# Attention on one core: later split subtractions on GpSimd, the transfers around the reciprocals issued a step later, the bias products ahead of the first projections

## The chip, the core and the metric

The kernel runs on one core of a Trainium2 chip. A core has TensorE (PE in the profile, matmul), VectorE (DVE), ScalarE (ACT), GpSimd (POOL) and SyncE (SP), which here only starts transfers. Each engine works through its own instructions in order and waits on semaphores for the others. Transfers are started from an engine's queue and carried out by 16 DMA engines. The metric is device time in microseconds of one execution.

## The reference, cut to what matters

Four layers follow each other on an input of 8 images, 256 channels, 32 x 32 pixels. The change lies in the first one, an attention block with an MLP:

```python
y = _bn(xf, g1, b1)                       # batch norm over images and pixels
q = einsum('bcn,oc->bon', y, wq) + bq     # 16 heads, 16 channels each
k = einsum('bcn,oc->bon', y, wk) + bk
v = einsum('bcn,oc->bon', y, wv) + bv     # 16 heads, 64 channels each
attn = softmax(einsum('bhnk,bhkm->bhnm', q, k) / KD ** (-0.5))
o = einsum('bhnm,bhmd->bhnd', attn, v)
o = einsum('bdn,od->bon', o, wp) + bp
xf = xf + o
# then a batch norm, an MLP with relu6 and a residual
```

There are 1024 pixels, so each head of each image has a 1024 x 1024 matrix of scores. The other layers (a deformable convolution, a binary convolution, another deformable convolution) are computed after it by code that the change does not touch.

## The kernel before, in words

**Groups, blocks and steps.** Heads are taken four at a time: a *group* is an image b and a quarter g of the heads, 32 groups in all. A group's queries are halved; a *block* is (b, g, half), 64 in all. A block runs over eight *steps*, one per tile of 128 keys. `step(t)` issues for every t: the scores of the next step and their exponentials (`exps`, L451 and L452), the products of the current step's exponentials with v (`attend`, L463), the running sum of the exponentials on GpSimd (L471 and L473, two instructions of 128 x 1024 a step; none at a block's first key tile), and the search for the largest score of a block 11 steps ahead (`score_max`, L406 products and L410 maxima).

**What else falls into a step.** `plan(step, place, f, ...)` puts a piece of other work into a step at place 0, 1 or 2, and within a place in the order of the calls. The manual schedule holds PE, ACT, DVE and POOL to the written order. SP is not among these engines; its transfers stand in an order that the framework chooses, and the trace shows some of them ahead of ones written earlier.

**Split levels.** The largest score is found from products in bf16. So q and k are each split into three bf16 levels whose sum is the f32 value. `project_qk` (L333 to L349) projects one half of q or k for two groups, copies the result to u (ACT, L346), sends it to DRAM as u_d (L347) and rounds it to level 0 (ACT, L348). `split` then makes, at stage 0, the rest (DVE, L357), at stage 1 level 1 (ACT, L362), and at stage 2 level 2 (DVE, L364); each level goes to DRAM as lev_d (L349, L365). There are four such projections per pair of groups, at steps 8, 10, 12 and 14 of the even group; their stage 2 stands at steps 11, 14, 16 and 18, place 0. The tile u has two buffers and `lev` four. `stack` (L372) gathers levels back from lev_d into sq and sk, 32 transfers per group, half of them for a first pair of heads ("pair 0"); `spread` (L378) brings u_d into q and k.

**Row sums and reciprocals.** When a block has ended (t1_ is its first step after), the sums over keys are made by a product with ones: `total` at t1_ + 3 (L484, copied by ACT at L491). It also starts four transfers that lay the four rows of 512 out as 128 x 16 (L494). `invert` at t1_ + 6 takes the reciprocal (DVE, L497) and sends it to DRAM as inv_d (L499). `lay` at t1_ + 8 reads it back, broadcast over partitions (L506), and `scale` at t1_ + 10 multiplies the block's output on GpSimd (L511). `add_projected` (L541 to L549) projects it and adds it to x. Block 62 has smaller offsets. The last block is done by `total_last` and `scale_last`, with no transfers.

**The largest score.** `enter_max` (L424 to L439) turns a block's maxima into a row of the queries, 11 steps before the block ends, by DVE and four transfers.

**The head.** After the input has landed and its batch norm statistics are made, four normalisations (L315) on DVE, four projections and four v projections are issued, then the splits and stacks of the first group; its two halves of u and its transfers to q and k alternate between SP and POOL. Steps -11 to -4 hold the search for the first block's maxima, which uses f32 products (`score_max_first`, L419, with maxima at L422). `bias(t)` adds the projection of bv to bp: eight products of one column (L305) and an add (L306), for t = 0 and 1. They are planned at steps -6 and -4:

```python
for t in range(2):
    plan(2 * t - 6, 1, bias, t)
```

Of the kernel before, what the change touches and what calls it, by code (L numbers as in the profile page):

```python
# [8 lines left out]
F32 = mybir.dt.float32  # L9
# [9 lines left out]
P = 128  # L19
# [3 lines left out]
HALF = N // 2  # L23
# [135 lines left out]
def conv_seq_kernel(ctx: ExitStack, tc: tile.TileContext, d: dict, out: bass.AP):  # L159
    nc = tc.nc  # L160
# [19 lines left out]
    def col(name, i=0, n=1, p=P):  # L180
        o = COL[name] + i
        return vec[:p, o : o + n]
# [53 lines left out]
    with ExitStack() as s0:  # L236
# [30 lines left out]
        sp = s0.enter_context(tc.tile_pool(name="a_s", bufs=2))  # L267
# [13 lines left out]
        for dst, name, scale in ((bq4, "bq", 4.0), (bk, "bk", 1.0)):  # L281
            ps = ps_p.tile([P, 512], F32, name="pb")
# [12 lines left out]
        def bank():  # L295
            return ps_p.tile([P, 512], F32, name="pb")
# [5 lines left out]
        def bias(t):  # L302
            ps = bank()
            for i in range(8):
                nc.tensor.matmul(ps[:, 0:1], wp[:, i, t * P : (t + 1) * P], bv[:, i : i + 1], start=i == 0, stop=i == 7)  # L305
            nc.vector.tensor_add(bpv[:, t : t + 1], ps[:, 0:1], col("bp", t))  # L306
# [3 lines left out]
        def normed(b, t, h):  # L310
            if t == h == 0:
                ys[b] = yp.tile([P, 2, N], F32, name="y")
            cols = slice(h * HALF, (h + 1) * HALF)
            if b == 0:
                nc.vector.tensor_scalar(ys[b][:, t, cols], x[:, t, b, cols], s1[:, t : t + 1], t1[:, t : t + 1], ALU.mult, ALU.add)  # L315
            else:
                nc.scalar.activation(ys[b][:, t, cols], x[:, t, b, cols], AF.Identity, bias=t1[:, t : t + 1], scale=s1[:, t : t + 1])
# [4 lines left out]
        def project_qk(b, g2, i):  # L322

            if i == 0:
                u_d[b, g2] = ld.tile([2, P, N], F32, name="u_d")
                lev_d[b, g2] = ld.tile([2, 3, P, N], BF16, name="lev_d")
            which, h = QK[i]
            wt, scale, bias = ((wq, 4.0, bq4), (wk, 1.0, bk))[which]
            cols = slice(h * HALF, (h + 1) * HALF)
            ps = bank()  # L330
            for t in range(2):
                for c in range(2):
                    nc.tensor.matmul(  # L333
                        ps[c * 64 : (c + 1) * 64, :], wt[:, t, g2 * P + c * 64 : g2 * P + (c + 1) * 64], ys[b][:, t, cols],
                        start=t == 0, stop=t == 1,
                    )
            if (b, g2) == (0, 0):

                both = ep.tile([P, 2, HALF], F32, name="e")
                u, rest = both[:, 0, :], both[:, 1, :]  # L340
                lev = ap.tile([P, 2, HALF], F32, name="esum").rearrange("p a c -> p (a c)").bitcast(BF16)
                lev = [lev[:, k * HALF : (k + 1) * HALF] for k in range(3)]
            else:
                u = rest = qp.tile([P, HALF], F32, name="u")
                lev = [lp.tile([P, HALF], BF16, name="lev"), None, None]
            nc.scalar.activation(u, ps, AF.Identity, bias=bias[:, g2 : g2 + 1], scale=scale)  # L346
            nc.sync.dma_start(u_d[b, g2][which, :, cols], u)  # L347
            nc.scalar.copy(lev[0], u)  # L348
            nc.sync.dma_start(lev_d[b, g2][which, 0, :, cols], lev[0])  # L349
            parts[i] = u, rest, lev  # L350

        def split(b, g2, i, stage):

            which, h = QK[i]
            u, rest, lev = parts[i]
            if stage == 0:
                nc.vector.tensor_sub(rest, u, lev[0])  # L357
                return
            if lev[stage] is None:
                lev[stage] = lp.tile([P, HALF], BF16, name="lev")  # L360
            if stage == 1:
                nc.scalar.copy(lev[1], rest)  # L362
            else:
                nc.vector.tensor_sub(lev[2], rest, lev[1])  # L364
            nc.sync.dma_start(lev_d[b, g2][which, stage, :, h * HALF : (h + 1) * HALF], lev[stage])  # L365

        def stack(b, g, pair, i, engines=(nc.sync, nc.sync)):
# [110 lines left out]
        rows, inv_d = {}, {}  # L478

        def totals(m):  # L480

            ps = bank()
            for j in range(4):
                nc.tensor.matmul(ps[32 * j : 32 * j + 32, :], ones[:, 0:32], sums[m, j // 2][:, j % 2, :], start=True, stop=True)  # L484
            return ps

        def total(m):

            ps = totals(m)
            row = sp.tile([P, HALF], F32, name="r", bufs=1)  # L490
            nc.scalar.copy(row, ps)  # L491
            rows[m] = sp.tile([P, 16], F32, name="r16")
            for j in range(4):
                nc.sync.dma_start(rows[m][32 * j : 32 * j + 32, :], row[32 * j : 32 * j + 1, :].rearrange("o (p c) -> o p c", c=16))  # L494

        def invert(m):
            nc.vector.reciprocal(rows[m], rows[m])  # L497
            inv_d[m] = ld.tile([4, HALF], F32, name="inv_d")
            nc.sync.dma_start(inv_d[m].rearrange("j (p c) -> (j p) c", c=16), rows[m])  # L499

# [61 lines left out]
        def plan(step, place, f, *args):  # L562
            work.setdefault((step, place), []).append(lambda: f(*args))

        for n, (b, g) in enumerate(groups):
# [14 lines left out]
            if n % 2 == 0 and n + 2 < len(groups):  # L580
                b_, g2 = groups[n + 2][0], groups[n + 2][1] // 2
                for i in range(4):
                    plan(t0 + 8 + 2 * i, 1, project_qk, b_, g2, i)
                    at = t0 + (10, 12, 15, 17)[i]
# [3 lines left out]
        for n, m in enumerate(blocks):  # L588
            b, g, h = m
            t1_ = (n + 1) * NT  # L590
            if m == blocks[-1]:
                plan(t1_, 0, total_last, m)
                plan(t1_ - 4, 0, make_pick)
                for pair in range(2):
                    plan(t1_ + 5 + pair, 0, scale_last, m, pair)
            else:
                plan(t1_ + 3, 1, total, m)
                at = 6 if n + 2 == nblk else 8
                plan(t1_ + (5 if at == 6 else 6), 0, invert, m)
                plan(t1_ + at, 2, lay, m)  # L600
                for pair in range(2):
                    plan(t1_ + at + 2, pair, scale, m, pair)
            for t in range(2):
                at = (7, 10) if m == blocks[-1] else (9, 10) if m == blocks[-2] else (13, 15)
                plan(t1_ + at[t], 1, add_projected, b, g, t, h)
            if m == blocks[-1]:
                plan(t1_ + 1, 0, nc.scalar.activation, w.tile([P, 1], F32, name="root"), eps, AF.Sqrt)
            plan(t1_ - AHEAD, 0, enter_max, m)
        for t in range(2):
            plan(2 * t - 6, 1, bias, t)  # L610

        def step(t):
            ne, nm = divmod(t + 1, NT), divmod(t + AHEAD, NT)
# [18 lines left out]
        with tc.manual_schedule(engines={mybir.EngineType.PE, mybir.EngineType.Activation, mybir.EngineType.DVE, mybir.EngineType.Pool}):  # L632
            for t in range(2):
                for h in range(2):
                    normed(0, t, h)

            nc.scalar.dma_start(wv, d["wvT"].rearrange("(t p) o -> p t o", p=P))
            nc.gpsimd.dma_start(wp, d["wpT"].rearrange("(t p) o -> p t o", p=P))
            nc.gpsimd.dma_start(bv, d["bv"].rearrange("(t p) -> p t", p=P))
            for i in range(4):  # L640
                project_qk(0, 0, i)
                which, h = QK[i]
                for j in range(4):
                    dst = (qs, ks)[which][0][32 * j : 32 * j + KD, h * HALF : (h + 1) * HALF]
                    (nc.gpsimd if j % 2 else nc.sync).dma_start(dst, parts[i][0][j * KD : (j + 1) * KD, :])
                split(0, 0, i, 0)
            for i in range(4):
                project_v(0, 0, i)
                split(0, 0, i, 1)
                split(0, 0, i, 2)  # L650
            for pair in range(2):
                for i in range(8):
                    stack(0, 0, pair, i, (nc.sync, nc.gpsimd))
            for t in range(-AHEAD, steps + 2 * NT):
                step(t)
            assert not work
# [6 lines left out]
    with ExitStack() as s1_:  # L663
# [334 lines left out]
        for b in range(B):  # L998
            r = 100 * b
# [18 lines left out]
            r = 100 * b - 50  # L1018
# [12 lines left out]
            for t in range(NT):  # L1031
# [8 lines left out]
                if t % 2:  # L1040
                    u = t // 2
# [31 lines left out]
    with ExitStack() as s3_:  # L1073
# [55 lines left out]
        def bank3():  # L1129
            return pp.tile([P, 512], F32, name="ps")  # L1130
# [17 lines left out]
            ps=2, pc=1, pd=1, pw=3, pa=1,  # L1148
# [264 lines left out]
        for b in range(B):  # L1413

            r = 100 * b
# [64 lines left out]
            r = 100 * b + 150  # L1480
# [35 lines left out]
        ps = bank3()  # L1516
# [8 lines left out]
    with tc.If(nc.values_load(flag[0:1, 0:1]) > 0):  # L1525
        with ExitStack() as s3_:
# [17 lines left out]
            first = w.tile([P, GK], F32, name="first")  # L1544
# [220 lines left out]
```

## Time and profile before

| what | value |
|---|---|
| median of three runs | 4542.85 us (4538.98 to 4544.85) |
| the profiled execution's own time | 4529.35 us |
| its span, first to last instruction | 4527.5 us |
| PE busy | 4008.4 us, 89% of the span |
| GpSimd busy | 3301.9 us, 73% |
| VectorE busy | 2863.6 us, 63% |
| ScalarE busy | 1874.9 us, 41% |
| L364, third level, on VectorE | 60 in the loop, 1593 ns mean |
| L357, rest, on VectorE | 60 in the loop, 1137 ns mean |
| L511, scaling, on GpSimd | 126, 1335 ns mean |
| L473, running sum, on GpSimd | 762, 2405 ns mean |

The span includes everything from the first instruction to the last. Attention takes from about 37 us to about 2685 us of it. Shares of busy time are averages over stages with different limits. A wait is listed as "engine, what waited, its line, <- who released it, what, its line", with the total time, the number of waits and the longest. An instruction that waits for several semaphores is put down to the last that came. In lists in order of time the first two columns are start and duration; neighbours of one kind are merged ("x10"), and square brackets hold the idle time of the engine before the instruction and what ended it. "SPq" and "POOLq" are the engines' queues, where transfers are issued; the time shown there is that of the issue, not of the transfer.

### The profile page before, as it was taken

What the parts mean: (1) busy time and instruction counts of PE and PEld (TensorE: products, weight loads), DVE (VectorE), ACT (ScalarE), POOL (GpSimd) and SP (SyncE); (2) the same over time, 40 slices, a digit from 0 to 9 for tenths busy, and PEclk for the clock granted to TensorE, in tenths of its full rate; (3) what the DMA queues carried; (4) which work ended last, traced back from release to release, by engine and by line L of the source; (5) the groups of instructions that cost most, each with busy time, mean ns of one, the idle gap of its engine ahead of it and who ended that gap; (6) DMA issues with size and microseconds to landing.
All of it is one profiled execution on the core that took longest, in us unless ns stands there. A gap on an engine that the chain in (4) does not pass through costs nothing.

```text
span 4527.5 us, 59803 instructions
## 1 busy us (share of the span) xinstructions
PE 4008.4 (89%) x20879; PEld 1528.1 (34%) x20879; DVE 2863.6 (63%) x4984; ACT 1874.9 (41%) x3360; POOL 3301.9 (73%) x2011
## 2 busy tenths in 40 slices
PE   6999999999999999999999997767767757899976
PEld 2333333333333333333333333323223222344332
DVE  5666666666666666666666663455455444688885
ACT  2554555555555555555555541122212211534331
POOL 2889888888889888888888863455555453078787
PEclk8999999999999999999999998788888778999978
DMA  5222221121221222122122112222223222100000
GB/s 163 66 60 54 68 71 54 59 76 55 66 67 54 61 71 65 53 63 75 53 64 68 54 50 63 73 84 79 81 85 93 81 86 69 47 10 15 14 15 24
DMA packets 224358, 284.11 MB, mean 63 GB/s; under 512 B 104352, under 2 KB 134576, under 8 KB 223792
## 3 DMA queue, kind: packets, MB, share of 16 engines
q1 hardware_dynamic: 193488, 196.49, 15.0%
q0 software_dynamic: 28720, 77.90, 5.8%
q10 hardware_dynamic: 1840, 5.81, 0.3%
q8 instruction: 168, 2.75, 0.3%
q14 instruction: 142, 1.16, 0.1%
HBM read 214.10 MB, written 64.34 MB: 62 GB/s over the span
## 4 chain that ended last, share of the span: by engine, by line
PE 73%; DVE 6%; another core or an unknown queue 6%; POOL 5%; issue 5%; DMA 2%; ACT 2%; SPq 1%; DVEq 0%; POOLq 0%; ACTq 0%
PE av L463 18%; PE sc L451 11%; PE pb L406 11%; PE pb L389 5%; PE pb L541 5%; PE pm L758 4%; PE po L771 3%; PE pc L1188 3%; PE pb L333 2%; POOL part L1387 2%; PE pc L978 2%; PE pb L484 1%; POOL ws L1331 1%; PE pa L1379 1%
## 5 line engine op out<-in xcount | busy, mean ns | idle before, releaser
L410 DVE TENSOR_REDUCE pm<-pb 128x1 f32<-128x512 f32 x2016 | 1375.7, 688 | 799.2 <-PE pb L406 796.2
L473 POOL TENSOR_TENSOR esum<-esum,e 128x1024 f32<-128x1024 f32 x762 | 1808.7, 2405 | 58.7 <-ACT e L452 57.5
L452 ACT ACTIVATE e<-sc 128x512 f32<-128x512 f32 x2048 | 1056.9, 602 | 653.2 <-PE sc L451 647.4
L463 PE MATMUL av<-e,v 128*64 128x512 f32 x4096 | 1051.1, 593 | 0.0
L891 POOL DMA_INDIRECT g<-table,idx x576 | 550.0, 955 | 551.2 <-DVE near_p L913 253.9
L406 PE MATMUL pb<-sk,sq 128*64 128x512 bf16 x4032 | 769.0, 387 | 42.8 <-ACT u L346 19.8
L451 PE MATMUL sc<-q,k 32*128 32x512 f32 x4096 | 591.4, 641 | 0.0
L406 PEld LDWEIGHTS <-sq 128*64 128x64 bf16 x4032 | 247.6, 109 | 877.6 <-issue 844.6
L471 POOL TENSOR_TENSOR esum<-e 128x1024 f32<-128x1024 f32 x127 | 303.1, 2406 | 277.7 <-ACT e L452 277.7
L758 PE MATMUL pm<-y,wide 128*128 128x512 f32 x512 | 262.3, 657 | 141.3 <-ACT hid L763 112.4
L463 PEld LDWEIGHTS av<-e,v 128*64 128x64 f32 x4096 | 289.9, 137 | 239.9 <-issue 146.9
L1387 POOL TENSOR_TENSOR part<-part,pr 128x512 f32<-128x512 f32 x212 | 276.0, 1302 | 55.0 <-DVE pr L1370 43.9
L1370 DVE TENSOR_TENSOR pr<-pw,v 128x512 f32<-128x512 f32 x394 | 253.8, 682 | 61.7 <-POOL part L1387 31.8
L1188 PE MATMUL pc<-xpad,wc 128*128 128x512 f32 x576 | 276.4, 605 | 5.3 <-ACT h L1193 5.3
L771 PE MATMUL po<-hid,w 128*128 128x512 f32 x512 | 241.9, 618 | 5.1 <-issue 4.0
L541 PE MATMUL pb<-o,wp 128*64 128x512 f32 x1024 | 244.7, 597 | 0.5 <-DVE r L519 0.3
L451 PEld LDWEIGHTS sc<-q,k 32*128 32x128 f32 x4096 | 164.4, 183 | 231.1 <-issue 187.3
L389 PE MATMUL pb<-wide,y 128*64 128x256 f32 x2048 | 241.8, 379 | 0.0
L763 ACT ACTIVATE hid<-pm,vec 128x512 f32<-128x512 f32 x128 | 87.1, 686 | 311.8 <-PE pm L758 140.8
L765 DVE TENSOR_SCALAR hid<-hid 128x512 f32<-128x512 f32 x128 | 53.1, 432 | 253.1 <-ACT hid L763 222.3
L758 PEld LDWEIGHTS pm<-y,wide 128*128 128x128 f32 x512 | 104.0, 210 | 279.7 <-issue 153.1
L913 DVE TENSOR_TENSOR near_p<-g,near_p 128x320 f32<-128x320 f32 (+1 forms) x384 | 177.4, 462 | 13.2
(259 smaller groups left out, 3981.7 us busy)
## 6 DMA issues: line engine op xcount, KB each, us to landing
sq<-lev_d SPq DMA_DIRECT2D x512, 64.0 KB
r<-inv_d SPq DMA_DIRECT2D x252, 128.0 KB
sk<-lev_d SPq DMA_DIRECT2D x496, 64.0 KB
lev_d<-lev SPq DMA_DIRECT2D x180, 128.0 KB
u_d<-u SPq DMA_DIRECT2D x60, 256.0 KB
g<-table,idx POOLq DMA_INDIRECT x576
table<-v SPq DMA_DIRECT2D x32, 256.0 KB
out<-res SPq DMA_DIRECT2D x32, 256.0 KB
```

The costliest lines, as they stand in the source:

```text
L389: nc.tensor.matmul(ps[c * 64 : (c + 1) * 64, (mt % 2) * 256 : (mt % 2 + 1) * 256], ys[b][:, t, k0 : k0 + 64], wv[:, t, g * 256 : (g + 1) * ...
L406: nc.tensor.matmul(ps[c * 64 : (c + 1) * 64, :], sq[pair][:, c, q0 : q0 + 64], sk[pair][:, c, kh * HALF : (kh + 1) * HALF], start=True, st ...
L410: nc.vector.tensor_reduce(maxima[m][:, pair, qt, kh : kh + 1], ps, AX.X, ALU.max)
L451: nc.tensor.matmul(ps, k[r, kt * P : (kt + 1) * P], q[r, h * HALF : (h + 1) * HALF], start=True, stop=True)
L452: nc.scalar.activation(es[m, kt, j // 2][:, j % 2, :], ps, AF.Exp)
L463: nc.tensor.matmul(av[i * HD : (i + 1) * HD, :], vss[b, g][:, kt, j * HD : (j + 1) * HD], e[:, i, :], start=kt == 0, stop=kt == NT - 1,)
L473: eng.tensor_add(sums[m, pair], sums[m, pair], es.pop((m, kt, pair)))
L541: nc.tensor.matmul(ps[c * 64 : (c + 1) * 64, :], wp[:, 2 * g + i, o0 : o0 + 64], outs[(b, g, h), i], start=i == 0, stop=i == 1,)
L758: nc.tensor.matmul(ps, w1[:, t, i * P : (i + 1) * P], ys[b, h][:, t, :], start=t == 0, stop=t == 1)
L771: nc.tensor.matmul(pss["o", b, h, t], w2[:, j, t * P : (t + 1) * P], hids[b, h, j], start=j == 0, stop=j == 7)
L891: nc.gpsimd.indirect_dma_start(out=g[:, k, :], out_offset=None, in_=tables[b][:TR, :], in_offset=bass.IndirectOffsetOnAxis(ap=idxs[b][:, t ...
L1188: nc.tensor.matmul(S["c", b, h], wc[:, t, k, :], tap(xpads[t], k, H // 2, h * H // 2), start=t == k == 0, stop=t == 1 and k == 8,)
```

## The change

Stage 2 of every split (the subtraction that makes level 2) runs on GpSimd. For the first pair of groups alone, stage 0 does too. `total` now ends with ACT's copy; the four row transfers are in a new function, `narrow`, planned a step later, at t1_ + 4, place 2. `invert` ends with the reciprocal; its transfer to DRAM is in a new function, `put`, planned a step before `lay`, at t1_ + 7, place 2 (t1_ + 5 for block 62). `invert` and `lay` keep their steps. The two calls of `bias` are made in the head, after the transfers of the weights are issued and ahead of the first projection.

```diff
@@ split
+            first = (b, g2) == (0, 0)
             if stage == 0:
-                nc.vector.tensor_sub(rest, u, lev[0])
+                (nc.gpsimd if first else nc.vector).tensor_sub(rest, u, lev[0])
                 return
...
             else:
-                nc.vector.tensor_sub(lev[2], rest, lev[1])
+                nc.gpsimd.tensor_sub(lev[2], rest, lev[1])
@@ total, invert
         def total(m):
             ps = totals(m)
-            row = sp.tile([P, HALF], F32, name="r", bufs=1)
-            nc.scalar.copy(row, ps)
+            rows[m] = sp.tile([P, HALF], F32, name="r", bufs=1)
+            nc.scalar.copy(rows[m], ps)
+
+        def narrow(m):
+            row = rows[m]
             rows[m] = sp.tile([P, 16], F32, name="r16")
             for j in range(4):
                 nc.sync.dma_start(rows[m][32 * j : 32 * j + 32, :], row[32 * j : 32 * j + 1, :].rearrange("o (p c) -> o p c", c=16))
 
         def invert(m):
             nc.vector.reciprocal(rows[m], rows[m])
+
+        def put(m):
             inv_d[m] = ld.tile([4, HALF], F32, name="inv_d")
             nc.sync.dma_start(inv_d[m].rearrange("j (p c) -> (j p) c", c=16), rows[m])
@@ the plan of a block
                 plan(t1_ + 3, 1, total, m)
                 at = 6 if n + 2 == nblk else 8
+                plan(t1_ + 4, 2, narrow, m)
                 plan(t1_ + (5 if at == 6 else 6), 0, invert, m)
+                plan(t1_ + at - 1, 2, put, m)
                 plan(t1_ + at, 2, lay, m)
@@ after the blocks
-        for t in range(2):
-            plan(2 * t - 6, 1, bias, t)
@@ the head
             nc.gpsimd.dma_start(bv, d["bv"].rearrange("(t p) -> p t", p=P))
+            for t in range(2):
+                bias(t)
             for i in range(4):
                 project_qk(0, 0, i)
```

## The prediction

> **What bounds the kernel now.** I read the windows of the span first, then who waited for whom on TensorE (PE), then the instructions in order of time around each kind of wait, and last the head. In the windows (microseconds; busy time and instruction count of PE, its weight loads, VectorE, ScalarE, GpSimd; granted clock; DMA share; GB/s) two stretches of the attention stage stand for all of it:
>
> ```profile
> 400.00:800.00 400.00, 394.59 (x2530) 141.69 (x2528) 262.99 (x430) 211.12 (x398) 351.76 (x159) 1.00 0.22 63
> 800.00:1600.00 800.00, 786.01 (x5032) 282.26 (x5030) 530.38 (x857) 423.07 (x797) 700.63 (x314) 1.00 0.22 62
> ```
>
> PE is busy 98.3% of the 800 us at full clock, so nothing but PE's own gaps can be won there: 14 us in 800. GpSimd is next, 88%, and the change gives it more. PE's waits between 90 and 2560 us (total, times, longest):
>
> ```profile
> PE pb L406 <- ACT u L346: 19.8, 15, 1.4
> PE pb L406 <- DMA sk<-lev_d: 10.2, 7, 1.8
> PE pb L406 <- DMA sq<-lev_d: 9.7, 7, 1.5
> PE pb L406 <- DMA q<-u_d: 1.3, 1, 1.3
> ```
>
> That is one wait of each of two kinds in each of the 15 pairs of head groups (163 us a pair): A, a score product waits for the copy of a projection (19.8 us in all), and B, it waits for stacked levels to land (21.2 us). How A comes about, in the pair that starts near 297 us (start, duration, what, and in brackets the idle time before it and its releaser):
>
> ```profile
> 310.39 24.53 POOL L473 TENSOR_TENSOR esum<-esum,e 128x1024 f32<-128x1024 f32 x10
> ...
> 329.83 2.88 DVE L364 TENSOR_TENSOR lev<-u,lev 128x512 bf16<-128x512 f32 x1
> 332.80 0.69 ACT L346 ACTIVATE u<-pb,bq 128x512 f32<-128x512 f32 x1 [3.97 <-DVE lev L364]
> 333.54 0.41 PE L406 MATMUL pb<-sk,sq 128*64 128x512 bf16 x2 [1.36 <-ACT u L346]
> ```
>
> The fourth projection's u takes the buffer (two of them) that the second split still reads at L364, and L364 takes 2.88 us. It is not the work that takes so long:
>
> ```profile
> L364 DVE TENSOR_TENSOR lev<-u,lev x60: 800/1526/2898, 155.5 to 2470.5; 128x512 bf16<-128x512 f32 x60
> L364 DVE TENSOR_TENSOR esum<-e,esum x4: 692/693/694, 49.2 to 54.4; 128x512 bf16<-128x512 f32 x4
> ```
>
> (min/median/max ns.) The four of the head, where GpSimd adds nothing, take 0.69 us; those beside its adds up to 2.9. B, in the same pair:
>
> ```profile
> 359.75 2.46 SPq L494 DMA_DIRECT2D r<-r  x4
> 362.26 0.58 SPq L372 DMA_DIRECT2D sq<-lev_d  x1
> 362.89 0.42 SPq L372 DMA_DIRECT2D sk<-lev_d  x1
> ...
> 365.65 0.41 PE L406 MATMUL pb<-sk,sq 128*64 128x512 bf16 x2 [1.40 <-DMA sq<-lev_d]
> ```
>
> SyncE's queue (SPq) stood from 356.6 to 359.75 for the totals (row of L491), issued their four transfers, and only then the last two of the 16 stacks of pair 0, which PE needs at 364.25. In the head, VectorE's maxima of the first block:
>
> ```profile
> 70.02 0.68 DVE L422 TENSOR_REDUCE pm<-sc 128x1 f32<-128x512 f32 x1
> 72.92 0.16 DVE L306 TENSOR_TENSOR bpv<-pb,vec 128x1 f32<-128x1 f32 x1 [2.22 <-PE pb L305]
> 74.92 0.69 DVE L422 TENSOR_REDUCE pm<-pb 128x1 f32<-128x512 f32 x1 [1.84 <-PE sc L419]
> ```
>
> Maxima otherwise follow each other at 0.60 us within a step and 1.05 between steps. Each of the two bias products, 3.5 us of PE, opens a gap of 4.90.
>
> **The skill beside it.** The page "SBUF — State Buffer", section "Who interferes with whom", says that a VectorE instruction with two SBUF inputs shares a read port with a GpSimd instruction that reads SBUF, and that the later one waits for the whole of the earlier. The rows of L364 agree: 2.88 is 0.69 plus most of one 2.32 us add, and the ten adds took 24.53 where ten clean ones take 23.2. The forecast goes by the rows. The rule says the move to GpSimd takes L364 out of that contest, while the other subtraction, L357, stays in it. For the price of a subtraction on GpSimd, "GPSIMD Engine Reference", section 3.1, gives about 2.6 cycles an element, 1.1 us for 512 at 1.2 GHz (an estimate from that page) without dispatch; the trace has a nearer row, below, which I use.
>
> **Third-level subtractions on GpSimd (60 in the loop).** No GpSimd instruction with a bf16 operand and two inputs is in the trace. The nearest is the scaling L511: 128x512, two f32 inputs, min 1.254, median 1.270 us. I take 1.25. From below 1.1 (the page); from above 2.4, the price of a 128x1024 add, if mixed types halve the rate (a bf16 memset of 2304 elements takes 2.02 us and an f32 one of 1152 takes 1.06, so memset shows no such penalty). Walk GpSimd's queue in the pair above, with clean adds of 2.32: the adds of key tile 3 run 310.39 to 315.03; subtraction 0 to 316.28; tile 4 to 320.92, plus 0.45 for L357 (the 1.35 us excess of ten adds over three such VectorE instructions) is 321.37; tile 5 to 326.01; tile 6 to 330.65; subtraction 1 to 331.90. So u starts at 331.9 rather than 332.80. PE was ready at 332.18 and u takes 0.69 with 0.05 to be seen, so 331.44 would be early enough: 0.48 of the 1.36 us stays and 0.88 goes. Fourteen pairs give 12.3 and the first, whose wait was 0.78 and whose GpSimd queue has no scaling in it, all 0.78: **13 us of A's 19.8**. Each 0.1 us on the subtraction costs 0.2 us a pair, as two stand ahead of u. Subtraction 2 falls into the 5.42 us in which GpSimd waits for the next block's exponentials, free. Subtraction 3 stands behind the adds of tile 2, near 352.2 where L364 ended near 354.0; the scalings behind it move by 1.25 and the block's last add by the same, into 4.5 us of idle before the next block. The exponentials' buffers (six tiles, three steps) come free 5 us or more before they are wanted. The 120 us of added queue is thus hidden but for the 0.48.
>
> **Row transfers and reciprocals.** SP is not held to the written order; the trace shows it ordered by readiness, with written order as the tie-break (stacks written after the totals stand before them). With the four row transfers written after step 3's stacks, the last two stacks go out at about 356.6, right behind the four before them, and land some 2 us after their issue, 4 us or more before PE wants them: **B goes, 21 us**. The rows then go out at 359.75 or a microsecond later, land by 363, and the reciprocal comes near 374.4: 11 us of cover. The output of the reciprocals (L499) stood in front of ten stacks of pair 1 and held the queue for it; a step later it stands behind them. The broadcast reads (L506) must wait for it to land, about 2 us. In the first block of a pair they went at 302.11, behind the next projection's u_d, and 302.11 + 2.67 + 2 is 306.8 against the scaling at 307.47: cover 0.7 us, the thinnest in the change. The write of the reciprocals now follows the stacks at about 295.2 and lands by 297.5, still before 301, so I price it at nothing. No instruction on VectorE moves: the reciprocal keeps its place, only its transfer is later.
>
> **Head.** Taking the bias products out closes 4.90 - 0.60 = 4.30 and 4.90 - 1.05 = 3.85: 8.15 us. Put ahead of the projections, their weights have landed (GpSimd's queue q0 moved its last bytes by 20 us); the two PSUM banks come free at 31.3 (L288), so two times 3.5 us of PE lie between 31.3 and 38.3, where PE waited until 37.01 for VectorE. Their adds (L306) come behind the four normalisations that end at 38.23, so the first projection starts near 38.4, 1.4 us later. It ran at half pace at first (eight products 3.7 us, later eight 1.9): if the bias products already wake the clock the delay comes back, if not it stays. I take half: **7.4 us** net. The first-level subtractions of the head and its GpSimd transfers now share one queue (four of 1.25, four pairs of transfers of 1.0), ending about 1 us later than before; the stacks then land near 74, wanted near 77. DVE, freed of both, starts its maxima no later than before.
>
> **Sum.** 13 + 21 + 7.4 = 41 us. The profiled execution took 4529.35 us (span 4527.5); it would take 4488. It lies 13.5 below the median of the runs, 4542.85; 41 off that median gives **4502**.
>
> **Rivals.** 1, the tie stays: the totals remain ahead of the last stacks because in the chosen order subtraction 3 on GpSimd counts as late. For it: the third level of q does hang on that subtraction. Against it: it is done 2 us earlier. B stays, 41 - 21 = 20: 4522. 2, the subtraction costs 1.6 to 2.4 us. A's wait is then 1.2 to 2.8 us a pair: gain 41 - 2 x 15 x (0.35 to 1.15) = 30 to 6, so 4512 to 4536. 3, slower: the broadcast reads slip behind the second projection's u_d (310.28) since they now hang on a later write. They would go at 311, 9 us later, land at 315.6, and GpSimd, in order, stands at the scaling for 8 us with all of the block's adds and two subtractions behind it; u and PE follow by as much. 15 x 8 - 41: +79, 4622. It decides from a slip of 0.7 + 41/15 = 3.4 us on. Against it: a whole projection stands between, and before the change the reads never slipped that far. 4, the gains are eaten by new small waits: 4543.
>
> **Chances.** Forecast 0.60 (its own range 4490 to 4513, from 1.1 to 1.5 us a subtraction and 6.5 to 9 in the head); rival 1 0.13; rival 2 0.10; rival 4 0.05; rival 3 0.12. The measurement tells 0.2% (9 us) from no change. Faster 0.83, same 0.05, slower 0.12. The range, 4488 to 4530, takes in rival 1 and most of 2.
>
> **What would show it.** Right: PE's waits on u fall to some 7 us, those on sq and sk to near nothing; a GpSimd group of 64 subtractions at 1.25 us; L422's maxima without the two gaps. Wrong: GpSimd idle in front of its scalings for DMA; subtractions over 1.6 us; row transfers still in front of the last two stacks.

## The result and the profile after

The changed kernel is slower: 4603.25 us median of 4 runs (4597.26 to 4606.04) against 4542.62 for the kernel before on the same chip (4 runs, 4538.98 to 4544.85). The ratio is 1.0132, with an interval of 1.0115 to 1.0150. The forecast was 4502.

The loss arises in attention. The first product of the MLP (L758 before, L768 after) starts at 2690.9 us before and at 2750.8 after, 59.9 later; the medians differ by 60.6. (The two profiled spans, 4527.5 and 4595.5 us, differ by 68.0; the other 8 us lie in the layers behind attention.) Line numbers move with the edit: L365 becomes L367 (a level's transfer to DRAM), L364 becomes L366 (its subtraction), L439 becomes L441 (the row of maxima into q, "q<-line"), L451 becomes L453 (score products of `exps`), L494 becomes L499 (row transfers).

PE's waits of after between 90 and 2560 us (total, times, longest):

```profile
PE sc L453 <- DMA q<-line: 42.6, 15, 3.1
```

That is the whole list. Waits A and B, the two kinds that the prediction was about, are gone entirely. One new kind is there, again once in each of the 15 pairs: the score products of a new block wait for the row of maxima that `enter_max` puts into q. In the window of after from 800 to 1600 us, beside the one shown of before, PE is as busy as it was (785.51 of 800 us), yet does fewer products (4890 for 5032) at a mean granted clock of 0.98 for 1.00:

```profile
800.00:1600.00 800.00, 785.51 (x4890) 281.19 (x4888) 491.38 (x813) 413.97 (x775) 697.55 (x327) 0.98 0.21 62
```

The reason stands in SP's queue. First the kernel before, in order of time, in the pair that starts near 297 us:

```profile
324.54 0.86 DVE L432 STREAM_TRANSPOSE line<-nm 32x32 f32<-32x32 f32 x4
324.98 2.82 SPq L439 DMA_DIRECT2D q<-line  x4
...
331.04 1.14 PE L451 MATMUL sc<-q,k 32*128 32x512 f32 x8
...
332.73 0.34 SPq L365 DMA_DIRECT2D lev_d<-lev  x1
```

The row goes out as soon as VectorE has made it, and the second projection's level 2 goes out 8 us later, when its subtraction is done. Now the same place in the kernel after:

```profile
320.79 9.93 SPq L367 DMA_DIRECT2D lev_d<-lev  x2
...
323.28 0.86 DVE L434 STREAM_TRANSPOSE line<-nm 32x32 f32<-32x32 f32 x4
...
329.23 1.15 POOL L366 TENSOR_TENSOR lev<-u,lev 128x512 bf16<-128x512 f32 x1
329.47 0.38 PE L408 MATMUL pb<-sk,sq 128*64 128x512 bf16 x2
...
330.81 2.82 SPq L441 DMA_DIRECT2D q<-line  x4
...
332.70 4.15 PE L453 MATMUL sc<-q,k 32*128 32x512 f32 x8 [2.85 <-DMA q<-line]
...
336.79 0.64 PE L408 MATMUL pb<-sk,sq 128*64 128x512 bf16 x2
...
337.21 1.92 PE L465 MATMUL av<-e,v 128*64 128x512 f32 x4
```

The two transfers of L367 now stand ahead of the four of L441 in SP's order. The second of them carries the level that GpSimd makes, behind its running sums, at 329.23 to 330.38. So the row, complete at 324.14, leaves from 330.81 on. PE's next products in order after 329.85 are the score products. It waits 2.85 us for the first transfer to land, then starts them two by two as the four transfers arrive, and each runs at half pace (1.05 to 1.19 us instead of 0.59 to 0.69). By both the eight take 4.15 us, where they take 1.14 together otherwise. The products behind them are slow too (0.64 for two that usually take 0.41, 1.92 for four that usually take 1.02). The granted clock shows why: it is 0.50 from the end of the wait to about 339.1, so 6.8 us of each pair's 167 run at half pace, which is the drop of the mean to 0.98. Windows of after, columns as above:

```profile
325.00:329.85 4.85, 4.85 (x30) 1.48 (x24) 2.71 (x5) 2.06 (x4) 4.85 (x3) 1.00 0.00 0
332.70:339.00 6.30, 6.29 (x16) 2.69 (x18) 0.69 (x1) 2.39 (x4) 2.27 (x1) 0.50 0.37 111
```

SP's own waits show the held transfer without a timeline. Of before:

```profile
SPq L365 <- DVE lev L364: 105.2, 44, 3.8
SPq L365 <- DVE r L497: 57.6, 15, 4.1
```

The second row is, by the times of the pair near 297 us, projection 1's level: the reciprocal that VectorE makes just behind its subtraction came last by the profile. The two together are 162.8 us in 59 waits. Of after:

```profile
SPq L367 <- POOL lev L366: 237.5, 60, 9.2
```

### The profile page after: what moved, and what is told of

It is laid out like the page before. It is cut to its first block, busy times and chain, and to the rows that moved or that the text cites. A ratio compares the mean times of both kernels' runs of the same rounds, so it can differ in the third digit from the quotient of the medians.

```text
span 4595.5 us, 59727 instructions
## 1 busy us (share of the span) xinstructions
PE 4066.4 (88%) x20879; PEld 1547.1 (34%) x20879; DVE 2780.2 (60%) x4916; ACT 1881.0 (41%) x3360; POOL 3348.0 (73%) x2079
## 4 chain that ended last, share of the span: by engine, by line
PE 73%; another core or an unknown queue 7%; POOL 6%; DVE 5%; issue 5%; ACT 2%; DMA 1%; SPq 0%; DVEq 0%; POOLq 0%; ACTq 0%
PE av L465 19%; PE sc L453 13%; PE pb L408 11%; PE pb L391 5%; PE pb L548 5%; PE pm L768 3%; PE pc L1198 3%; PE po L781 3%; POOL part L1397 2%; PE pb L333 2%; PE pc L988 1%; PE pb L486 1%; DVE near_p L923 1%; POOL ws L1341 1%
## 5 line engine op out<-in xcount | busy, mean ns | idle before, releaser
L475 POOL TENSOR_TENSOR esum<-esum,e 128x1024 f32<-128x1024 f32 x762 | 1788.8, 2380 | 62.9 <-ACT e L454 62.4
L465 PE MATMUL av<-e,v 128*64 128x512 f32 x4096 | 1066.6, 602 | 0.0
L453 PE MATMUL sc<-q,k 32*128 32x512 f32 x4096 | 636.4, 653 | 42.6 <-DMA q<-line 42.6
L768 PE MATMUL pm<-y,wide 128*128 128x512 f32 x512 | 260.1, 652 | 145.8 <-ACT hid L773 121.0
L453 PEld LDWEIGHTS sc<-q,k 32*128 32x128 f32 x4096 | 186.6, 186 | 286.5 <-issue 197.8
L768 PEld LDWEIGHTS pm<-y,wide 128*128 128x128 f32 x512 | 102.6, 208 | 283.2 <-issue 146.1
L988 PE MATMUL pc<-xb,ws 128*128 128x512 bf16 x504 | 132.0, 421 | 71.0 <-ACT ac L999 36.2
```

What stands on the lines that cost most here:

```text
L453: nc.tensor.matmul(ps, k[r, kt * P : (kt + 1) * P], q[r, h * HALF : (h + 1) * HALF], start=True, stop=True)
L465: nc.tensor.matmul(av[i * HD : (i + 1) * HD, :], vss[b, g][:, kt, j * HD : (j + 1) * HD], e[:, i, :], start=kt == 0, stop=kt == NT - 1,)
L475: eng.tensor_add(sums[m, pair], sums[m, pair], es.pop((m, kt, pair)))
L768: nc.tensor.matmul(ps, w1[:, t, i * P : (i + 1) * P], ys[b, h][:, t, :], start=t == 0, stop=t == 1)
```

## The experiments

The theory (T) after reading the traces: the loss is the place of one transfer in SP's queue. Projection 1's level 2 waits for GpSimd, and the row of maxima waits behind it. Rivals: the row transfers that now go out later push something else back (X); or GpSimd's added work itself holds up the rest, whatever SP's order (G).

The runs come from several chips, on which the layers after attention run at different granted clocks (0.85 in `before` and 0.94 in `bias`, from 2800 to 4150 us); the kernel before takes 4543, 4211 or 4528 us. The expectations of `bias`, `xfer`, `split` and `poolq` give whole times, to be read as differences from 4543. Each time below is a difference from the kernel before on the same chip, and beside it stands the start of the MLP's first product in that run's trace, which marks the end of attention (2690.9 before, 2750.8 and 2755.4 in two profiles of after).

| kernel | us against before | ratio and interval | end of attention |
|---|---|---|---|
| `bias`: bias products alone | -5.4 | 0.9988 (0.9981 to 0.9995) | 2684.5 |
| `xfer`: row transfers alone | -23.7 | 0.9946 (0.9929 to 0.9962) | 2666.8 |
| `split`: subtractions alone | +84.6 | 1.0202 (1.0185 to 1.0219) | 2777.6 |
| `again`: the change once more | +59.8 | 1.0122 (1.0092 to 1.0153) | 2755.4 |
| `nosplit`: the change without the subtractions | -29.0 | 0.9931 (0.9914 to 0.9947) | 2661.1 |
| `only_i1`: before, one subtraction of four moved | +68.1 | 1.0163 (1.0146 to 1.0180) | 2757.8 |
| `poolq`: the change, one transfer in GpSimd's queue | -37.9 | 0.9911 (0.9895 to 0.9928) | 2652.5 |
| `actq`: the change, that transfer in ScalarE's queue | -48.6 | 0.9882 (0.9866 to 0.9899) | 2641.8 |
| `i1_dve`: the change, one subtraction back on VectorE | -48.0 | 0.9890 (0.9874 to 0.9907) | 2641.1 |
| `dose`: the change, that one subtraction done twice | +98.1 | 1.0186 (1.0144 to 1.0228) | 2777.9 |

### The three parts alone

`bias` is the kernel before with this edit:

```diff
-        for t in range(2):
-            plan(2 * t - 6, 1, bias, t)
...
+            for t in range(2):
+                bias(t)
             for i in range(4):
                 project_qk(0, 0, i)
```

> The kernel before with one edit of the change: the bias products ahead of the first projections. Nothing in the loop over pairs differs, the transfer to q<-line stands in SP's queue as before. Every theory expects the same here, 4535 us (4533 to 4538): the first score product of exps came 7.7 us earlier in the changed kernel (83.06 against 90.78 us), and that carries to the end. If it shows 4540 or more, the head's gain does not reach the end, and the loss in the loop is smaller than reckoned.

Measured: -5.4 us, at the edge of what was expected. The first score product of `exps` starts at 85.5 us, not at 82.99 as in the changed kernel: alone, the edit wins 5.3 us there. The expectation had set down to it all that the changed kernel gains there, 7.8 us (its 83.06 is the time at which a list of the chain of work has that step; the product itself starts at 82.99).

`xfer` is the kernel before with `narrow` and `put`:

```diff
-            row = sp.tile([P, HALF], F32, name="r", bufs=1)
-            nc.scalar.copy(row, ps)
+            rows[m] = sp.tile([P, HALF], F32, name="r", bufs=1)
+            nc.scalar.copy(rows[m], ps)
+
+        def narrow(m):
+            row = rows[m]
...
+        def put(m):
...
+                plan(t1_ + 4, 2, narrow, m)
...
+                plan(t1_ + at - 1, 2, put, m)
```

> The kernel before with one edit of the change: narrow and put, the transfers around the reciprocals, issued a step later. Theory T (the loss is the level transfer of projection 1, which now waits for GpSimd ahead of the q<-line transfer in SP's queue): the subtractions are still on VectorE, so nothing is lost, and wait B (21.2 us in the kernel before) goes: 4521 us (4515 to 4530). Rival X (the later transfers push the loads of the next pair back): 4600 us or more, with the wait of the score product on q<-line in this trace too. Rival G (GpSimd's added load) expects the same as T here.

Measured: -23.7 us. PE's waits on sq and sk are gone, A is there as before (19.8 us in 15 waits), q<-line does not show. X is out.

`split` is the kernel before with the subtractions moved:

```diff
-                nc.vector.tensor_sub(rest, u, lev[0])
+                (nc.gpsimd if first else nc.vector).tensor_sub(rest, u, lev[0])
...
-                nc.vector.tensor_sub(lev[2], rest, lev[1])
+                nc.gpsimd.tensor_sub(lev[2], rest, lev[1])
```

> The kernel before with one edit of the change: the split's late subtractions on GpSimd. Theory T: all of the loss is here. 15 pairs lose about 7.2 us each at the score product that waits for q<-line (108 us) and win wait A (13 to 20 us): 4543 + 108 - 17 = 4634 us, 4620 to 4640; with B still there one of the two waits may shorten the other, which is why the low end is 4620. Rival X: 4525 us, as forecast for the subtractions alone. Rival G (POOL busier, whatever the order of SP's queue): 4620 to 4640 as T; the next kernel parts these two.

Measured: +84.6 us, inside the expected +77 to +97; the loss is in this part. PE's largest wait between 80 and 2720 us:

```profile
PE sc L452 <- DMA q<-line: 44.3, 16, 3.3
```

A is gone here, and half of B as well (10.9 us of 19.9 are left in its waits on sq and sk); PE comes later to it.

> The changed kernel itself, beside which the next one is read. The parts measured alone were -5.4 us (bias products), -23.7 (row transfers) and +84.6 (subtractions); if they add up, 55.5 us above the kernel before, 50 to 62.

Measured: +59.8 us, where the three parts add up to 55.5, inside the interval of 42 to 69 us. The parts are not quite independent: `split` and `xfer` both shorten B.

> The changed kernel with all subtractions back on VectorE: bias products and row transfers as changed. If the parts add up: the 5.4 us of the bias products alone and the 23.7 us of the row transfers alone, 29 us below the kernel before (24 to 33).

`nosplit` has the edits of `bias` and `xfer` together. Measured: -29.0 us, as expected, with A still there (19.7 us).

### Order of the queue, or load of GpSimd

`only_i1` moves a quarter of the work, in the kernel before:

```diff
-                nc.vector.tensor_sub(lev[2], rest, lev[1])
+                (nc.gpsimd if i == 1 and (b, g2) != (0, 0) else nc.vector).tensor_sub(lev[2], rest, lev[1])
```

> The kernel before with one subtraction of the four on GpSimd: projection 1's level 2. The head and the row transfers are as before. SP's order of issue flips as in the changed kernel: projection 1's level-2 transfer ahead of q<-line. Theory T: nearly the whole loss of the split with a quarter of its work on GpSimd: 70 to 105 us above the kernel before. Rival G: a quarter of the split's +85, about +20.

Measured: +68.1 us (61 to 76 from the interval), at the low end of what T expects (just under its 70) and over three times what G does. SP's queue of this kernel (the list ends at 340 us, with three of the row's four transfers):

```profile
328.59 9.50 SPq L365 DMA_DIRECT2D lev_d<-lev  x2
...
336.58 1.16 POOL L364 TENSOR_TENSOR lev<-u,lev 128x512 bf16<-128x512 f32 x1
...
338.18 2.13 SPq L439 DMA_DIRECT2D q<-line  x3
```

It is the pattern of after with one GpSimd subtraction a pair. PE's wait on q<-line is 33.0 us in all (2.2 a pair), 11 less than in `split`, where more subtractions stand in GpSimd's queue; that is 11 of the 16.5 us between the two kernels.

`i1_dve` is the complement: in the changed kernel the same one goes back, the other three stay on GpSimd.

```diff
-                nc.gpsimd.tensor_sub(lev[2], rest, lev[1])
+                (nc.vector if i == 1 and not first else nc.gpsimd).tensor_sub(lev[2], rest, lev[1])
```

> The changed kernel with one of the four subtractions back on VectorE: that of projection 1's level 2 (in the loop; the head keeps the change). GpSimd keeps three of the four, and both other edits stay. In SP's order of issue the q<-line transfers then stand ahead of projection 1's level-2 transfer again. Theory T: the loss is gone: 15 to 35 us below the kernel before (head 6, B 24, and A only as far as the other three subtractions caused it). Rival G (GpSimd's added work): three quarters of the loss stays, 35 to 60 us above the kernel before.

Measured: -48.0 us, more than T asked for and opposite to G. SP's queue has the row ahead again, and PE is without a gap over 800 us and more (windows of `i1_dve`, columns as above):

```profile
317.21 2.83 SPq L441 DMA_DIRECT2D q<-line  x4
...
323.28 1.14 PE L453 MATMUL sc<-q,k 32*128 32x512 f32 x8
...
323.32 0.34 SPq L367 DMA_DIRECT2D lev_d<-lev  x1
```

```profile
800.00:1600.00 800.00, 800.00 (x5128) 285.07 (x5126) 519.31 (x856) 432.97 (x813) 726.07 (x336) 1.00 0.22 64
```

Why more: I had kept part of A. But A is gone as well (one wait of 1.2 us), though projection 1's subtraction is back on VectorE beside GpSimd's adds. It takes 1.34 us on average there. In the kernel before it took (60 x 1.593 - 45 x 1.159) / 15 = 2.90, with the 1.159 from `only_i1`, where the other three alone are on VectorE. In the pair near 297 us of before it starts at 329.83, together with an add of GpSimd (329.82 to 332.15), and ends 2.88 later; in `i1_dve` it starts at 322.07, toward the end of an add (320.39 to 322.74), and ends 1.22 later. Both end about 0.55 us after that add. That its length depends on where in an add it falls is read from these rows; no run tried it by itself.

### The transfer alone

`poolq` and `actq` leave all arithmetic of the change where it is and move only the issue of projection 1's level-2 transfer.

```diff
@@ poolq
-            nc.sync.dma_start(lev_d[b, g2][which, stage, :, h * HALF : (h + 1) * HALF], lev[stage])
+            eng = nc.gpsimd if stage == 2 and i == 1 and not first else nc.sync
+            eng.dma_start(lev_d[b, g2][which, stage, :, h * HALF : (h + 1) * HALF], lev[stage])
```

```diff
@@ actq
+            if stage == 2 and i == 1 and not first:
+                return
             nc.sync.dma_start(lev_d[b, g2][which, stage, :, h * HALF : (h + 1) * HALF], lev[stage])
...
+        def send(b, g2, i):
+            which, h = QK[i]
+            nc.scalar.dma_start(lev_d[b, g2][which, 2, :, h * HALF : (h + 1) * HALF], parts[i][2][2])
...
+                    if i == 1:
+                        plan(t0 + 14, 2, send, b_, g2, i)
```

> The changed kernel with the one transfer moved: the level-2 transfer of projection 1 (not of the first, in the head) is issued from GpSimd's own queue, behind its subtraction, and so no longer stands in SP's queue ahead of the q<-line transfer. GpSimd does the same arithmetic and has 15 transfers to issue on top. Theory T: the wait of the score product on q<-line goes, and the time is what the prediction expected of the change, 4502 us, 4495 to 4515. Rival G (GpSimd's added load itself, through its adds or through SBUF): 4595 us or more, no better than the change. Rival X: 4595 us or more as well, as the later transfers are all still there.

Measured: -37.9 us; the forecast for the change was -41. The wait on q<-line is gone from PE's list.

> The changed kernel with projection 1's level-2 transfer issued from ScalarE's queue, at a step of the plan of its own, in place of SP's. Theory T: the wait on q<-line goes here as it went with GpSimd's queue: 25 to 40 us below the kernel before. It may lose part of that, since ScalarE stands at the issue until GpSimd's subtraction is done, and the copies u and the exps behind it stand as well: if so, ScalarE shows in the waits of TensorE, up to 1 us a pair, 15 us. Rival G: 50 us or more above the kernel before.

Measured: -48.6 us, better than expected. ScalarE does stand at the issue, but only 3.2 us of waits on u are left in PE's list. GpSimd's work is all there, so G is out. In the pair near 297 us of `actq` the row leaves first and the level after it, from another queue, although GpSimd's subtraction starts 5.5 us after the row leaves (in after, 5.1 us after the row is complete):

```profile
315.18 2.82 SPq L447 DMA_DIRECT2D q<-line  x4
...
320.67 1.16 POOL L366 TENSOR_TENSOR lev<-u,lev 128x512 bf16<-128x512 f32 x1
...
322.58 0.35 ACTq L373 DMA_DIRECT2D lev_d<-lev  x1
```

`poolq` is 10.7 us behind `actq`. Each issue on GpSimd takes 0.59 us of that engine (15 of them, 8.9 us), and PE waits 6.5 us, in 14 waits, for VectorE's x (L557), a row that is not in the list of `actq`. The rows of the pair near 297 us lead from one to the other. GpSimd waits 0.30 us for its subtraction to be complete, then issues for 0.61, so its next two adds run 0.97 us later against the products (the second starts at 325.81; in `actq`, where the products are 0.75 us earlier here, at 324.09). VectorE's L359, which ends 0.55 us behind that add, takes 2.18 us for 1.21 in `actq`, and x stands behind it on VectorE. The pair near 480 us has the same (2.17 for 1.20, then 0.47 us of wait). The waits on x are 6.5 of the 10.7 us; the rest was not followed up.

### The cost doubled

```diff
-                nc.gpsimd.tensor_sub(lev[2], rest, lev[1])
+                for _ in range(2 if i == 1 and not first else 1):
+                    nc.gpsimd.tensor_sub(lev[2], rest, lev[1])
```

> The changed kernel with one suspected cost doubled: projection 1's level-2 subtraction (in the loop, 15 of them) is done twice over on GpSimd, 1.16 us more each, with the same result. It stands ahead of its transfer, and by theory T that transfer stands ahead of q<-line: every pair loses those 1.16 us more, 17 us in all (14 to 21), and the score product's wait on q<-line grows from 2.8 to 4.0 us a pair. If the wait on q<-line had another cause (the q<-line transfer itself being slow), GpSimd with its idle time would hide the extra work and the time would stay within 5 us of the changed kernel's.

Measured: the wait grows as expected, from 42.9 us (`again`) to 61.1, or 1.2 us a pair:

```profile
PE sc L454 <- DMA q<-line: 61.1, 15, 4.5
```

Attention ends 22.5 us later than in `again` (27 later than in the first profile of after), somewhat over the 14 to 21. The medians differ by 38, but the four times spread over 33 us (4601.7 to 4634.7), and 31 us of the profiled span's growth lie after attention, in layers that the edit does not touch; so the trace's figure is the one to use. Two profiles of the changed kernel differ by 4.6 us there, so the excess over 21 is not clear of noise.

## Why the prediction was wrong, point by point

**What bounds the kernel: right.** Only PE's gaps in attention could be won. With them closed (`i1_dve`), attention is 49.8 us shorter and PE is busy 800.00 of 800.

**Wait A: right in kind, too low in size.** A went. The subtraction on GpSimd takes 1.155 us (1.142 to 1.173), below the 1.25 assumed (by the prediction's rule of 0.2 us a pair for each 0.1, 0.19 us a pair):

```profile
L366 POOL TENSOR_TENSOR lev<-u,lev x60: 1142/1156/1173, 147.1 to 2529.6; 128x512 bf16<-128x512 f32 x60
```

Of the 19.8 us, 13 were forecast to go. With all four subtractions on GpSimd and SP's order mended, 3.2 are left (`actq`), so 16.6 go. Two slips of its sum change little: 331.90 less 331.44 is 0.46, not 0.48, and 60 subtractions of 1.25 us are 75 us of added queue (69.3 measured), not 120; none of its terms gives 120. Rival 2, a subtraction of 1.6 us or more, did not happen.

**Wait B: right.** 21 us forecast, -23.7 measured alone (-30 to -16 from the interval). In after the ten stacks go out in one run, the last at 361.11, and the rows behind them:

```profile
361.11 0.42 SPq L374 DMA_DIRECT2D sk<-lev_d  x1
...
364.11 2.46 SPq L499 DMA_DIRECT2D r<-r  x4
```

Rival 1, the tie that stays, is out. So is rival 3's slip: the broadcast reads (L513) go at 301.17 and the scalings start at 306.22 without a wait.

**Head: right in sum, not in how.** 7.4 us forecast; the first score product of `exps` starts 7.8 earlier (90.78, then 82.99). But the bias products did not bring the products behind them to full pace at all, where I had taken half. PE, in the kernel after:

```profile
31.51 6.99 PE L305 MATMUL pb<-bv,wp 128*128 128x1 f32 x32 [1.84 <-ACT bk L288]
38.56 3.68 PE L333 MATMUL pb<-y,wq 128*64 128x512 f32 x8
```

Eight products still take 3.68 us, as before. Alone, the edit therefore moves VectorE's first maximum from 55.02 to 57.44 and wins 8.15 - 2.42 = 5.7, of which 5.3 reach the score product. In after the maxima start at 55.39, since the split's subtractions no longer stand ahead of them on VectorE: 8.15 - 0.37 = 7.8. The sentence that VectorE, freed of both, starts no later was nearly right. The 7.4 came close by luck: the delay of the projections stayed whole (38.56 for 37.01), and the room that the subtractions left on VectorE made up for most of it.

**The step that failed.** The part on the subtractions walked through GpSimd's queue, followed each subtraction to u and to the stacks, and closed: "The 120 us of added queue is thus hidden but for the 0.48". A stage 2 issues two things, a subtraction and a transfer. The transfer stays in SP's queue, but what it waits for changed from VectorE to GpSimd, and I did not ask where SP would then have it, nor who stands behind it. The next part even said that "SP is not held to the written order"; it was applied to the row transfers alone. In the written order the row of maxima is a step ahead of this level; in the built kernel it comes behind. The rule of the prediction, readiness first, fails there too: the row is complete at 324.14 and the level at 330.38, and the level goes first. What made the framework choose this order no run shows.

The prediction's own numbers would have priced it. Its walk ends subtraction 1 at 331.90. In the trace of before the row goes out at 324.98 and PE wants it at 331.04. If the row goes out behind the level, from about 332.3 on, and lands some 2 us after its issue (the prediction's own figure for stacks), PE starts its first pair of products at 334.3, 3.3 us late; the fourth transfer is issued 2.1 us after the first (2.82 for four), so the last pair starts that much later as well, and the eight end about 5 us late. Fifteen pairs make 75 us of loss against 41 of gain: +34 at full pace, and +60 was measured, with the slow products on top (27 us by the estimate of 1.8 a pair below). It would have been a rival of the same kind as rival 3, a transfer held back behind one that hangs on something later, at another place in the same queue.

**The sum as measured.** With SP's order mended (`i1_dve`) attention is 49.8 us shorter: A 18.6 (19.8 to 1.2), B 21.2, head 7.8, together 47.6. The change gives back 109.7 (2750.8 less 2641.1), 7.31 a pair. In the pair near 297 us, from the last product on maxima before the block's first scores to the third behind them, after takes 10.60 us (329.47 to 340.07) and `i1_dve` 3.55 (322.97 to 326.52): 7.05, made up of 2.85 in the list of waits, 3.01 for the scores that come two by two at half pace (4.15 for 1.14), and 1.11 of slow products behind (3.28 for 2.17). Of the 3.01 the staggered arrival is the larger part: in a wait of `only_i1` whose scores run at full pace nearly to the end (last section) the eight take 3.44, 2.30 more than otherwise. By that row an estimate for the half pace is 0.71 + 1.11 = 1.8 us a pair, a quarter of the loss. The list of waits shows 42.6 us, two fifths of the loss.

## What to carry to other kernels

When work moves from one engine to another, follow its transfers too: a transfer in a shared queue holds everything behind it until its own data is there, so ask for each that now waits for a busier engine what stands behind it and how much slack that has. If the order of that queue is chosen by a framework, a new producer can change the order itself, and the written order is then no argument; in this case, `i1_dve` or `actq` keeps the gain and drops the loss (48 us below the kernel before, 0.989 and 0.988), by leaving that one subtraction on its engine or by giving that one transfer another queue.

## What the runs showed of the hardware

A wait of PE can cost more than its row: the granted clock falls to 0.50 about when PE stands, and stays there for 3.4 or 6.8 us. The windows of the profile give the times (an estimate where a window holds both clocks):

| wait of PE, until | its length, us | clock falls to 0.50 | and stays there, us |
|---|---|---|---|
| before, 333.54 and 365.65 (waits A and B) | 1.36 and 1.40 | not at all | |
| before, 853.80 (a wait B) | 1.83 | 0.1 us behind the wait | 3.4 |
| `only_i1`, 340.07 | 2.19 | 2.8 us behind the wait | 3.4 |
| `only_i1`, 506.41 | 2.16 | 0.4 us behind the wait | 6.8 |
| after, 332.70 | 2.85 | 0.5 us before its end | 6.8 |
| `dose`, 334.48 | 4.05 | 1.0 us behind the wait | 6.8 |

Length alone does not order these rows: two waits of 2.2 us in one kernel got one stretch of 3.4 us and one of 6.8, and the fall came 0.5 us before the end of the shorter of the last two waits and 1.0 us behind the longer. The two of `only_i1`, in order of time; in the first the products begin at full pace (0.66) and the eight end sooner:

```profile
340.07 3.44 PE L451 MATMUL sc<-q,k 32*128 32x512 f32 x8 [2.19 <-DMA q<-line]
...
506.41 4.18 PE L451 MATMUL sc<-q,k 32*128 32x512 f32 x8 [2.16 <-DMA q<-line]
```

The Trainium skill, "TensorE: Matmul & The Clock Gate", section "What's actually happening", has a busy monitor that halves the array's clock after an idle window of about 3.4 us. The halving agrees, and the stretches are one and two times that window; but here waits of 1.83 to 2.85 us, shorter than a window, were enough. No run tried it apart from the wait.

Seven us of one-column products (L305) left the products after them at half pace, as if PE had been idle: eight take 3.68 us with them ahead and without. This rests on the durations alone; the profile's granted clock reads 1.00 there in both kernels.

The Trainium skill, "DMA: Bandwidth & Descriptors", section "Issuing engines are not separate DMA queues", says that starting transfers from several engines saves only the time of issuing, usually small. For throughput no run here says otherwise; but a transfer that waits in the queue holds the ones behind it, and moving one issue in each of 15 pairs from SP to ScalarE was worth 109 us of attention (2750.8 to 2641.8).
